# Two tiles of a shared expert moved from a context stage into the following sums stage

## The chip, the cores and the metric

The kernel runs on one core of a Trainium2 chip. The metric is the device time of one execution in microseconds (us). The kernel before took 1562.98 us, the median of three runs that lie between 1562.39 and 1564.65.

## The reference, cut to what matters

The input is 4 sequences of 512 tokens with 512 channels. A half-weighted mixture-of-experts layer, attention, and the same mixture layer again are each added to the running sum:

```python
x = x + 0.5 * ffn(layernorm(x), ...)
x = x + attn(layernorm(x), ...)          # attn adds its own input once more
x = x + 0.5 * ffn(layernorm(x), ...)

# ffn, for the rows x of all 2048 tokens
router_logits = x @ gate_w                       # 64 experts
topk_w, topk_ids = grouped_topk(router_logits, bias)   # 6 experts of 4 of 8 groups
y = routed_moe(x, topk_w, topk_ids, w_gate, w_up, w_down)   # at most 96 tokens per expert
shared = silu(x @ ws_gate) * (x @ ws_up) @ ws_down          # 192 hidden channels, all tokens
return y + shared

# attn: 16 heads of 32 channels, rotary embedding on half of them
scores = einsum('bhqd,bhkd->bhqk', Q, K) / sqrt(32)
ctx = einsum('bhqk,bhkd->bhqd', softmax(scores), V)
return ctx @ W_out + X
```

The change concerns the line `shared`, in the second mixture layer, for one of the four sequences.

## The kernel before, in words

Everything is float32 in tiles of 128 rows; a sequence is four such tiles (TPB = 4). The kernel has three parts: the first mixture layer, the attention of the four sequences, and the second mixture layer with its 64 experts. Sequences are numbered from 0 in the code, so "the second sequence" is `b = 1`.

The attention part (the loop at L1066) has two stages for each sequence, a sums stage and a context stage, of 16 steps each.

- A step of `sums(b)` (L953 on) has four score matmuls `sc` (L962), two maxima on VectorE (L965), four exponentials with row sums on ScalarE (L970). From these the logarithm of each row's sum is formed (`logs`, L935), and transposed in `rows_of_sums` (`ps_m`, L980) at step 16.
- A step of `context(b)` (L1021 on) has four transposed score matmuls `sct` (L992) and four that subtract the logarithms (L996), two exponentials on ScalarE (`pT`, L1003), and the product with the values of the step before (`cx`, L1015).

Between these instructions the other work is threaded in. It stands in a list `work` of pairs, a number and a function (class `Pieces`, L44). Each step takes pieces off its head: `short()` takes a piece whose number is under 1.0, and it stands ahead of the step's exponentials; `long()` takes one short piece if one is at the head, and then one more of any size, behind the exponentials. In a sums stage `long` takes nothing once only two long pieces are left (`keep`), and `work.all()` puts out the rest between the stages, with no score matmuls beside it. `rest` is a long piece that does nothing. A second list, `work.later`, has small VectorE jobs; a sums step does one of them, a context step two.

What is threaded in: in the sums stage of `b`, the output projection of sequence `b-1` (`project`, `po`, L860) and the queries, keys and values of `b+1` (`qkv`, `pq`, L811); the fourth sums stage (`b = 3`) has no next sequence and takes routing work instead. The routing of a finished sequence consists of

- `early_rows` and `scored`: normalised rows `xn` (`route.row`, L295, stored to DRAM on the SP queue), their transposes (`route.turn`), and router scores `lg` (`route.score`, L308); after the last tile's score, the seven parts of `choices` (L319, VectorE, picks the experts) go to `work.later`;
- `gated`: for each of the four tiles, `route.gate` (four `gu` matmuls with the shared expert's weights, L208; a tanh on ScalarE, L211; two VectorE products, L214 and L215), `route.turn_h` (transposes of the hidden tile `sg`, L201, and a ScalarE copy `hT`, L202) and `route.down` (two `so` matmuls, L508, and a VectorE sum into `x`, L509). Tile i is turned and put down in the piece after the one that gates it, and `route.store` hands finished tiles to the SP queue (L516);
- `queued`: turns and puts down the fourth tile, does what is left of `choices`, then `count` (two `pp` matmuls, L405 and L406, that need the chosen masks `M` and `Ms` from VectorE), `digits` (VectorE), `tokens` (ScalarE, L436) and `spread` (`o` matmuls, L447), which build the experts' lists of tokens.

The order on PE, ScalarE and VectorE in this part is the order in which the code issues the work; each engine runs its own stream in order and waits by semaphores. Two pools of PSUM matter: `psS` with three buffers for `sc` and `sct` (a step uses two; in the second and third context stages `cx` takes one of the three), and `psT` with two buffers for all the other matmul results.

In the kernel before, all of sequence 1's routing (`scored(1)`, `gated(1)`, `queued(1)`) is threaded into the third context stage (`b = 2`); the fourth sums stage threads in the projection of sequence 2, two rests, and sequence 2's rows, scores and shared expert; the fourth context stage has two rests and `queued(2)`.

Of the kernel before, what the change touches and what calls it, by code (L numbers as in the profile page):

```python
# [21 lines left out]
TPB = S // P  # L22
# [61 lines left out]
def macaron_kernel(ctx: ExitStack, tc: tile.TileContext, X, ln_w, ln_b, W_in, W_out, gate_w, bias,  # L84
# [156 lines left out]
    def load_pair(layer, n, extra):  # L241


        slot = (extra if (n + (0 if layer else WS)) % (WS + WX) >= WS else wp).tile([P, 4608], F32, tag="w", name="w")
        wg = slot[:, 0:2 * DC * F].rearrange("p (t c f) -> p t c f", t=2, c=DC)
        wu = slot[:, 2 * DC * F:4 * DC * F].rearrange("p (t c f) -> p t c f", t=2, c=DC)
        wd = slot[:, 4 * DC * F:].rearrange("p (k d) -> p k d", k=3)
        two = slice(2 * n, 2 * n + 2)
        loaded[layer, n] = (wg, wu, wd)
        return [lambda: nc.sync.dma_start(wg, w_gate[two].rearrange("t (p c) f -> p t c f", c=DC)),  # L250
                lambda: nc.sync.dma_start(wu, w_up[two].rearrange("t (p c) f -> p t c f", c=DC)),
                lambda: nc.sync.dma_start(wd, w_down[two].rearrange("t f d -> (t f) d").rearrange("(k p) d -> p k d", p=P))]

    def load_now(*args):
        for go in load_pair(*args):
            go()
# [371 lines left out]
    with ExitStack() as s:  # L628
# [4 lines left out]
        with ExitStack() as f:  # L633
            rp = f.enter_context(tc.tile_pool(name="rp0", bufs=2))
            f.enter_context(tc.manual_schedule(engines={mybir.EngineType.SP}))
            xs = []
            for t in range(NT):
                g, i = divmod(t, TPB)
# [14 lines left out]
            for t in range(2 * TPB + 1):  # L653
                g, i = divmod(t, TPB)
# [14 lines left out]
            rest = [go for n in range(WS + WX) for go in load_pair(0, n, extra)]  # L669
# [58 lines left out]
    with ExitStack() as s:  # L728
# [8 lines left out]
        route = Route(1)  # L737
# [11 lines left out]
        xs, stats, qT, kT, v, nmT, keyed = xas, {}, {}, {}, {}, {}, {}  # L749
        work = Pieces()  # L750

        def places(b):
            qT[b] = qp.tile([P, DC, S], F32, tag="qT", name="qT")
            kT[b] = qp.tile([P, DC, S], F32, tag="kT", name="kT")
            v[b] = vp.tile([P, TPB, D], F32, tag="v", name="v")
# [17 lines left out]
        def summed(b):  # L773

            mv = small.tile([P, TPB, 2], F32, tag="mv4", name="mv")
            for i in range(TPB):
                stat_later(b, mv, i)
            steps_later(first(b, mv))
# [75 lines left out]
        def project(b):  # L854
            mv = small.tile([P, TPB, 2], F32, tag="mv4", name="mv")

            def part(q):
                po = psT.tile([P, 512], F32, tag="ps", name="po")
                for c in range(NC):
                    nc.tensor.matmul(po, lhsT=qT[b][:, c, q * P:(q + 1) * P], rhs=win[3][:, c, :],  # L860
                                     start=c == 0, stop=c == NC - 1)
                nc.vector.tensor_add(xs[b][q], xs[b][q], po)
                if b < B - 1:
                    stat_later(b, mv, q)
                    if q == TPB - 1:
                        steps_later(route.ready(b, mv))
            return [(3.4, lambda q=q: part(q)) for q in range(TPB)]

        def early_rows(b):
            def part(i):  # L870
                while (b, i) not in route.stats:
                    work.flush(1)
                route.row(b, xs[b], i)
            return [(0.1, lambda i=i: part(i)) for i in range(2)]

        rest = (1.0, lambda: None)

        def scored(b, chosen):

            def part(i):  # L880
                route.score(b, i)
                if i + 2 < TPB:
                    route.row(b, xs[b], i + 2)
                if i == TPB - 1:
                    steps = route.choices(b)
                    chosen.append(lambda: next(steps, None))
                    work.later[:0] = chosen * 7

            pieces = [(0.5, lambda: route.turn(b, 0)), rest]
            for i in range(TPB):  # L890
                if i + 1 < TPB:
                    pieces.append((0.5, lambda i=i: route.turn(b, i + 1)))
                pieces.append((1.4, lambda i=i: part(i)))
            return pieces

        def gated(b):
            def part(i):
                route.store()
                if i > 0:
                    route.down(b, xs[b], i - 1)  # L900
                route.gate(b, i)

            pieces = []
            for i in range(TPB):
                if i > 0:
                    pieces.append((0.3, lambda i=i: route.turn_h(b, i - 1)))
                pieces.append((4.3, lambda i=i: part(i)))
            return pieces

        def queued(b, chosen):  # L910

            def last():
                route.down(b, xs[b], TPB - 1)
                while work.later and work.later[0] in chosen:
                    work.flush(1)
                route.store()
                route.count(b)

            def digits(i):
                if i > 0:  # L920
                    route.spread(b, i - 2)
                route.digits(b, i)

            pieces = [(0.3, lambda: route.turn_h(b, TPB - 1)), (1.7, last)]
            for i in (0, 2):
                pieces += [(0.6, lambda i=i: digits(i)), (1.0, lambda i=i: route.tokens(b, i)), rest]
            pieces.append((0.6, lambda: route.spread(b, 2)))
            return pieces
# [109 lines left out]
        pieces, following = qkv(0), qkv(1)  # L1038
# [26 lines left out]
        chosen = []  # L1065
        for b in range(B):  # L1066
            if b > 0:
                pieces = project(b - 1)
                if b + 1 < B:
                    places(b + 1)  # L1070
                    following = qkv(b + 1)
                    pieces.insert(3, following.pop(0))
                    work.add(pieces + following[:-5] + early_rows(b - 1) + following[-5:])
                else:
                    work.add(pieces + [rest, rest] + early_rows(b - 1) + scored(b - 1, chosen) + gated(b - 1))
            logs = sums(b, work, 2)
            work.all()
            if b + 2 == B:
                load_now(1, 0, None)
            if b == 0:  # L1080
                summed(2)
                summed(3)
            elif b < B - 1:
                chosen = []
                work.add(scored(b - 1, chosen) + gated(b - 1) + queued(b - 1, chosen))
            else:
                work.add([rest, rest] + queued(b - 1, chosen))
            context(b, work, b in (0, B - 1), logs)
            work.all()
            chosen = []  # L1090
# [90 lines left out]
```

## Time and profile before

The profile is of one execution that took 1569.51 us; the span from its first to its last instruction is 1567.8 us. Busy time of the engines in the stages around the change, and the clock that TensorE was granted, as a share of full speed:

| stretch (us from the start) | stage | length | PE busy | DVE busy | ACT busy | PE clock |
|---|---|---|---|---|---|---|
| 766 to 847 | second context (`b = 1`) | 81 | 80.47 | 26.24 | 38.90 | 0.96 |
| 847 to 941 | third sums | 94 | 90.20 | 62.34 | 70.38 | 0.99 |
| 941 to 1020 | third context (`b = 2`) | 79 | 78.45 | 25.71 | 37.40 | 0.94 |
| 1020 to 1113 | fourth sums (`b = 3`) | 93 | 77.03 | 56.10 | 58.24 | 0.78 |
| 1113 to 1176 | fourth context | 63 | 60.62 | 16.45 | 34.59 | 0.92 |

PE is TensorE's matmuls, DVE is VectorE, ACT is ScalarE, SP is the queue that issues most transfers. A matmul's record is longer when the granted clock is lower, so "busy" grows without more work being done. In a timeline, a row merges neighbouring instructions of one line; a time in square brackets is how long the engine stood idle before the row, with the engine and line that ended the wait.

### The profile page before, as it was taken

To read this page: it belongs to the slowest core of one execution; us is meant where nothing else is said; L and a number is where in the kernel's file an instruction comes from. 1 tells how busy PE (TensorE), PEld (TensorE's weight loads), DVE (VectorE), ACT (ScalarE), POOL (GpSimd) and SP (SyncE) were. 2 spreads that over 40 slices of the span, in tenths; PEclk is the share of its full clock that TensorE was granted. 3 is DMA by queue.
4 is the path that set the end of the run, shared out by engine and by line. 5 is a ranking of instruction groups with operands and counts; after the bars stand their busy time and mean duration, and the time that the engine had idled before them with its cause. 6 is when DMAs were issued, how large, how long until landed. Compare 5 with 4: busy or idle time off the path is not lost.

```text
span 1567.8 us, 23011 instructions
## 1 busy us (share of the span) xinstructions
PE 1407.9 (90%) x9024; PEld 803.2 (51%) x9024; DVE 625.0 (40%) x1572; ACT 594.5 (38%) x1161; POOL 350.7 (22%) x321
## 2 busy tenths in 40 slices
PE   4785999999998998999999999978998899999990
PEld 4553777776753443334443434324334477777760
DVE  7575222211217566177144843375316422122110
ACT  4431121211112487668635774467362112121120
POOL 2001355545434000000000000000000245555535
PEclk9998899999999997999999998986798799999995
DMA  5477699999999300000000020000006389999989
GB/s 195 142 227 256 188 330 330 328 334 337 337 274 176 122 1 1 1 1 1 27 31 1 1 74 21 24 14 20 25 1 240 122 266 333 336 337 328 338 253 122
DMA packets 127036, 254.57 MB, mean 162 GB/s; under 512 B 15801, under 2 KB 32313, under 8 KB 126929
## 3 DMA queue, kind: packets, MB, share of 16 engines
q1 hardware_dynamic: 87216, 192.96, 35.1%
q0 software_dynamic: 39424, 59.97, 17.9%
q8 instruction: 72, 1.18, 0.3%
q14 instruction: 36, 0.29, 0.1%
q10 hardware_dynamic: 288, 0.16, 0.0%
HBM read 202.21 MB, written 56.95 MB: 165 GB/s over the span
## 4 chain that ended last, share of the span: by engine, by line
PE 56%; ACT 5%; DVE 4%; DMA 2%; issue 2%; POOL 1%; SPq 0%; POOLq 0%; ACTq 0%; DVEq 0%
PE pq L811 10%; PE gu L549 6%; PE sct L992 5%; PE sc L962 4%; PE cx L1015 4%; PE sct L996 4%; PE ps_t L201 4%; PE po L860 3%; PE eo L568 3%; PE gu L208 3%; PE so L508 3%; PE gu L553 3%; ACT sc L970 2%; PE eo L571 2%; DMA w<-in_L_ffn_w_up_dram 1%
## 5 line engine op out<-in xcount | busy, mean ns | idle before, releaser
L526 POOL DMA_INDIRECT xr<-xn_d,en x128 | 119.5, 934 | 893.7 <-DVE sg L215 721.2
L549 PE MATMUL gu<-bT,w 128*128 128x96 f32 x2048 | 245.1, 278 | 7.5 <-DMA w<-in_L_ffn_w_up_dram 7.3
L549 PEld LDWEIGHTS gu<-bT,w 128*128 128x128 f32 x2048 | 238.3, 194 | 10.3 <-issue 10.2
L970 ACT ACTIVATE sc<-sc,nmq 128x512 f32<-128x512 f32 x256 | 168.9, 660 | 58.2 <-DVE nmq L965 52.5
L811 PE MATMUL pq<-w,lT 128*128 128x512 f32 x384 | 177.1, 608 | 6.6 <-ACT lT L202 2.7
L965 DVE TENSOR_REDUCE nmq<-sc 128x2 f32<-128x1024 f32 x128 | 151.4, 1220 | 78.3 <-PE sc L962 78.2
L576 POOL DMA_INDIRECT total<-ob,en x96 | 138.6, 1443 | 159.3 <-ACT ob L575 120.4
L575 ACT ACTIVATE ob<-eo,xr 96x512 f32<-96x512 f32 x128 | 80.5, 678 | 185.9 <-PE eo L571 182.6
L560 DVE SCALAR_TENSOR_TENSOR sg<-sg,gu 128x288 f32<-128x288 f32 x64 | 29.0, 454 | 298.6 <-ACT sg L559 204.5
L1003 ACT ACTIVATE pT<-sct 128x1024 f32<-128x1024 f32 x128 | 124.1, 1023 | 58.1 <-PE sct L996 57.9
L559 ACT ACTIVATE sg<-gu 128x288 f32<-128x288 f32 x64 | 26.2, 410 | 314.4 <-PE gu L555 310.5
L568 PE MATMUL eo<-w,hT 128*96 128x512 f32 x256 | 125.3, 612 | 0.0
L202 DVE COPY bT<-ps_t 128x384 f32<-128x384 f32 x128 | 65.5, 552 | 147.4 <-PE ps_t L201 127.3
L811 PEld LDWEIGHTS pq<-w,lT 128*128 128x128 f32 x384 | 70.8, 193 | 95.9 <-issue 79.5
L962 PE MATMUL sc<-kT,qT 32*128 32x512 f32 x512 | 98.1, 719 | 10.4 <-ACT sc L970 9.8
L553 PE MATMUL gu<-bT,w 128*64 128x96 f32 x1024 | 99.9, 252 | 0.0
L555 PE MATMUL gu<-bT,w 128*64 128x96 f32 x1024 | 99.9, 252 | 0.0
L208 PE MATMUL gu<-wsgu,xT 128*128 128x384 f32 x256 | 94.8, 518 | 1.4 <-ACT ob L575 1.4
L992 PE MATMUL sct<-qT,kT 32*128 32x512 f32 x512 | 91.3, 659 | 2.1 <-ACT pT L1003 2.1
L553 PEld LDWEIGHTS gu<-bT,w 128*64 128x64 f32 x1024 | 87.7, 139 | 6.2 <-issue 0.3
L555 PEld LDWEIGHTS gu<-bT,w 128*64 128x64 f32 x1024 | 87.7, 139 | 0.0
L996 PE MATMUL sct<-nmT,pick 4*128 4x512 f32 x512 | 85.4, 614 | 0.0
(162 smaller groups left out, 1649.5 us busy)
## 6 DMA issues: line engine op xcount, KB each, us to landing
w<-in_L_ffn_w_gate_dram SPq DMA_DIRECT2D x64, 768.0 KB
w<-in_L_ffn_w_up_dram SPq DMA_DIRECT2D x64, 768.0 KB
w<-in_L_ffn_w_down_dram SPq DMA_DIRECT2D x64, 768.0 KB
total<-zero SPq DMA_DIRECT2D x39, 256.0 KB
xn_d<-xn SPq DMA_DIRECT2D x32, 256.0 KB
x<-in_L_attn_X_dram SPq DMA_DIRECT2D x16, 256.0 KB
x<-total POOLq DMA_DIRECT2D x16, 256.0 KB
out_dram<-x SPq DMA_DIRECT2D x16, 256.0 KB
```

Of the source, the lines that this page charges most:

```text
L208: nc.tensor.matmul(gu[:rows, :2 * F].rearrange("p (w f) -> p w f", w=2), lhsT=bT[:, c, :], rhs=weights[:, :, c, :], start=c == 0, stop=c = ...
L549: nc.tensor.matmul(g[:, k, :], lhsT=w[:, k, c, f:f + P], rhs=x[:, c, :], start=c == 0, stop=c == DC - 1)
L553: nc.tensor.matmul(g[:FC, 2, :], lhsT=w[:, 0, c, P:F], rhs=xa[:, c, :], start=c == 0, stop=c == DC - 1)
L555: nc.tensor.matmul(g[FC:, 2, :], lhsT=w[:, 1, c, 0:FC], rhs=xb[:, c, :], start=c == 0, stop=c == DC - 1)
L568: nc.tensor.matmul(eos[k][:CAP], lhsT=hT[:, k, :], rhs=wd[:, 2 * k, :], start=True, stop=False)
L576: nc.gpsimd.indirect_dma_start(out=total[layer][k], in_=ob, in_offset=None, out_offset=bass.IndirectOffsetOnAxis(ap=en[:, e:e + 1], axis=0 ...
L811: nc.tensor.matmul(pq, lhsT=lTs[i][:, c, :], rhs=win[n][:, c, :], start=c == 0, stop=c == DC - 1)
L962: nc.tensor.matmul(scs[j // 2][:, j % 2, :], lhsT=qT[b][rows, c, q * P:(q + 1) * P], rhs=kT[b][rows, c, :], start=True, stop=True)
L965: nc.vector.tensor_reduce(nmv[:, q, 2 * pair:2 * pair + 2, c], scs[pair], AX.X, ALU.max, negate=True)
L970: nc.scalar.activation(scs[j // 2][:, j % 2, :], scs[j // 2][:, j % 2, :], AF.Exp, bias=nmq[:, q, j * DH + c:j * DH + c + 1], accum_out=sm ...
L992: nc.tensor.matmul(scs[j // 2][:, j % 2, :], lhsT=kT[b][rows, c, kt * P:(kt + 1) * P], rhs=qT[b][rows, c, :], start=True, stop=False)
L996: nc.tensor.matmul(scs[j // 2][:, j % 2, :], lhsT=pick[rows, c, :], rhs=nmT[b][c // (NC - 1)][rows, :], start=False, stop=True)
```

## The change

The gates of the third and fourth tile of sequence 1, with the turning and putting down of its second, third and fourth tile, leave the third context stage and go into the fourth sums stage, directly behind the projection of sequence 2, in the place of the two rests. For that, `gated` takes a list of tiles, and has the turning and putting down of the fourth tile in itself (it was in `queued`). This last also holds for the other sequences: for sequence 0 in the second context stage, putting down the fourth tile and `count` become two pieces, in two steps; for sequence 2 the fourth tile is turned and put down in the fourth sums stage's list and no longer in the fourth context stage.

```diff
-        def gated(b):
+        def gated(b, tiles=range(TPB)):
             def part(i):
                 route.store()
                 if i > 0:
                     route.down(b, xs[b], i - 1)
                 route.gate(b, i)
 
+            def last():
+                route.down(b, xs[b], TPB - 1)
+                route.store()
+
             pieces = []
-            for i in range(TPB):
+            for i in tiles:
                 if i > 0:
                     pieces.append((0.3, lambda i=i: route.turn_h(b, i - 1)))
                 pieces.append((4.3, lambda i=i: part(i)))
-            return pieces
+            return pieces + ([(0.3, lambda: route.turn_h(b, TPB - 1)), (1.7, last)] if TPB - 1 in tiles else [])
 
         def queued(b, chosen):
 
             def last():
-                route.down(b, xs[b], TPB - 1)
                 while work.later and work.later[0] in chosen:
                     work.flush(1)
                 route.store()
...
-            pieces = [(0.3, lambda: route.turn_h(b, TPB - 1)), (1.7, last)]
+            pieces = [(1.0, last)]
...
-                    work.add(pieces + [rest, rest] + early_rows(b - 1) + scored(b - 1, chosen) + gated(b - 1))
+                    work.add(pieces + gated(b - 2, (2, 3)) + early_rows(b - 1) + scored(b - 1, chosen) + gated(b - 1))
...
-                work.add(scored(b - 1, chosen) + gated(b - 1) + queued(b - 1, chosen))
+                work.add(scored(b - 1, chosen) + gated(b - 1, range(TPB if b == 1 else 2)) + queued(b - 1, chosen))
```

No instruction of the kernel is added or taken away on TensorE, ScalarE, VectorE or the transfer queues; their order changes, and the queue of GpSimd keeps its order.

## The prediction

> **What bounds the kernel now.** First the page's busy shares and its row of slices, then the windows of the stages around the change:
>
> ```profile
> PE 1407.9 (90%) x9024; PEld 803.2 (51%) x9024; DVE 625.0 (40%) x1572; ACT 594.5 (38%) x1161; POOL 350.7 (22%) x321
> ...
> PEclk9998899999999997999999998986798799999995
> ```
>
> ```profile
> 941.00:1020.00 79.00, 78.45 (x486) 32.99 (x486) 25.71 (x81) 37.40 (x51) 0.00 (x0) 0.94 0.06 23
> 1020.00:1113.00 93.00, 77.03 (x266) 36.03 (x262) 56.10 (x95) 58.24 (x150) 0.00 (x0) 0.78 0.05 20
> 1113.00:1176.00 63.00, 60.62 (x428) 22.48 (x420) 16.45 (x53) 34.59 (x41) 0.00 (x0) 0.92 0.02 7
> ```
>
> PE sets the end everywhere but in the fourth sums stage (1020 to 1113): there it is idle for 16 of 93 us, and its clock is down to 0.78, while the third context stage (941 to 1020) keeps it busy for 78.45 of 79. So the change takes PE work out of a stage where PE is the bound and puts it where PE waits. How much of the idle time can be filled is seen in PE's timeline: first the steps of the third context stage with gated tiles, then the sums stage, then the start of the fourth context stage.
>
> ```profile
> 974.34 1.14 PE L992 MATMUL sct<-qT,kT 32*128 32x512 f32 x8
> 977.62 1.98 PE L508 MATMUL so<-wsd,hT 96*128 96x512 f32 x4
> 979.45 2.75 PE L208 MATMUL gu<-wsgu,xT 128*128 128x384 f32 x8
> 995.31 1.14 PE L992 MATMUL sct<-qT,kT 32*128 32x512 f32 x8
> ...
> 1038.49 1.99 PE L962 MATMUL sc<-kT,qT 32*128 32x512 f32 x12
> 1051.57 1.12 PE L201 MATMUL ps_t<-ident,xn 128*128 128x128 f32 x4 [3.87 <-ACT xn L295]
> 1080.22 4.14 PE L208 MATMUL gu<-wsgu,xT 128*128 128x384 f32 x8
> 1084.28 1.14 PE L962 MATMUL sc<-kT,qT 32*128 32x512 f32 x8
> 1090.93 1.14 PE L962 MATMUL sc<-kT,qT 32*128 32x512 f32 x8
> 1096.61 1.09 PE L980 MATMUL ps_m<-ident,nmq 128*128 128x128 f32 x4 [3.99 <-DVE nmq L950]
> 1105.53 0.43 PE L201 MATMUL ps_t<-ident,sg 128*96 128x128 f32 x2 [1.20 <-DVE sg L215]
> 1106.41 3.49 PE L508 MATMUL so<-wsd,hT 96*128 96x512 f32 x4 [0.46 <-ACT hT L202]
> 1112.60 1.14 PE L992 MATMUL sct<-qT,kT 32*128 32x512 f32 x8
> 1123.81 0.66 PE L201 MATMUL ps_t<-ident,sg 128*96 128x128 f32 x2
> 1126.27 2.44 PE L508 MATMUL so<-wsd,hT 96*128 96x512 f32 x4
> 1129.49 0.27 PE L405 MATMUL pp<-M,before 128*128 128x256 bf16 x1 [0.78 <-DVE x L509]
> ```
>
> Two steps are to be seen. The rests (from 1038.49) end in a wait of 3.87 us for the first normalised row, whose statistics are not ready; and from there on the same work takes longer: `gu` 4.14 us against 2.75, `so` 3.49 against 1.98. Windows cut at those places show why:
>
> ```profile
> 1059.00:1082.85 23.85, 22.53 (x80) 14.38 (x79) 11.08 (x12) 17.98 (x47) 0.00 (x0) 0.50 0.06 22
> 1082.85:1096.50 13.65, 9.06 (x37) 3.74 (x35) 11.53 (x33) 8.58 (x25) 0.00 (x0) 1.00 0.05 19
> 1117.00:1127.20 10.20, 10.20 (x39) 2.37 (x36) 2.02 (x9) 4.38 (x7) 0.00 (x0) 0.50 0.05 13
> ```
>
> The granted clock is 0.50 while rows are turned and scored, 1.00 while tiles are gated, and 0.50 again at the start of the context stage.
>
> **The change part by part** (times of the profiled execution).
>
> *Third context stage.* Before, three steps, from the `sct` at 974.34 to that at 995.31, hold what leaves (two `gu`, three turns, three `so`) and `count`: 20.97 us. After, one of them is left, with `sct` and `cx` (3.0 us, to 977.35) and `count`; `pp` waits for the masks, which VectorE's timeline has ready at 978.58 already now, so 1.1 us of waiting and 0.4 for `pp`: 4.4 us. Two plain steps come back at the end of the stage; such steps last 3.17 (995.31 to 998.48) and 3.83 us (to the `sct` at 1002.31), as PSUM holds only three `sct` buffers and `cx` has one: 7.0. With `choices` ending behind `count`'s wait, `digits` come 1.8 us later against the step, and `tokens` hold ScalarE for about 0.7. Gain: 20.97 - 4.4 - 7.0 - 0.7 = 8.9. Bounds: 8 (plain steps of 3.83 and twice the token wait) to 11 (plain steps of 3.04 as at 1156 to 1168 in the fourth context stage, no token wait).
>
> *Second context stage.* `count` moves to the next step; the last `spread` moves into the last step, where PE waits for the final exponentials anyway (0.18 at 843.50, and a `cx` of 1.97 us instead of 1.07). I take -0.5; bounds -1.2 (one whole `o` group, 1.09, hidden) and +1.5 (a `count` that waits as above).
>
> *Fourth sums stage, front.* Before, from the `sc` at 1038.49 to the first exponential behind the first row (ScalarE, 1051.32): 12.8 us. After, the two steps with a turn, `so` and `gu` last as the like step from 1084.28 to 1090.93, 6.65 each, PE-bound (ScalarE needs 2.95 + 0.37 + 0.33 in it, VectorE 2.4 + 1.4 + 0.9). The third has `sc`, turn, copy and `so` alone: 1.1 + 0.1 + 0.4 + 0.5 + 1.9 = 4.0. Then the eighth `sc` and its first maximum, and the row in front of its exponentials, 2.6 more; the statistics are done a step earlier, so no 3.87 wait. Sum 19.9: cost 7.0. The scoring steps that follow keep their period (6.02 us from the `sc` at 1061.14 to that at 1067.16), at half clock, since transposes and `lg` behind idle steps are what ran at 0.50 before. Bounds: 4.5 (turned rows start at full clock) to 8.5 (a third step of 5.5).
>
> *Its tail.* Before, from the second gate's end (1091.0) to the first `sct`, 1112.60: 21.6 us, with one sums step and a wait of 3.99 for the logarithms. After, one step of the stage fewer is left and one tile more. The logarithms stand behind the second gate's tanh and products: 0.35 + 0.75 + 0.45 = 1.6; `ps_m` 0.65; `sc` 1.1; then turn 0.55, copy 0.46, `so` and `gu` 4.6; twice wait for products 1.2, turn and copy 0.9, and `so` and `gu` 4.6, or `so` alone 2.0: 1.6 + 0.65 + 1.1 + 5.6 + 6.7 + 4.1 = 19.7. Half clock cost this tail 3.0 before (`sc` +0.95, `ps_m` +0.45, `so` +1.5, `gu` +0.2); I put half of it on: 21.2, a gain of 0.4. Bounds: -1.9 to +2.6 (two `so` more at 3.49).
>
> *Fourth context stage.* A turn, an `so` and the 0.78 wait of `pp` for its buffer go: 0.66 + 2.44 + 0.78 = 3.9. Four parts of `choices` instead of three stand behind the last sum `x`; they take 0.9 + 4.8 us (VectorE, 1102.02 to 1102.89 and 1113.73 to 1118.50), the log of the last column waits for them and the second exponentials for that: 0.7 given back. `count`, ten us behind the first `sct`, finds its masks (five us). Gain 3.1; bounds 2 to 6.3 (the third step, 9.7 us from 1120.08 to 1129.80, at 3.4 as with full clock).
>
> *Queues.* Three stores of `x` (256 KB or less each) now stand before sequence 2's row stores on SP, and the masks' weights `wt` before two of them; the transfers run at 20 GB/s in these stages, a row buffer is used again only two steps later, and the readers are the experts after 1243. Nothing, unless a row waited for its buffer: then 1 us at one step. POOL's order stays.
>
> Sum: -8.9 - 0.5 + 7.0 - 0.4 - 3.1 = -5.9. Behind the attention all shifts as it is. 1569.51 - 5.9 = 1563.6; the median of the runs is 0.9958 of the profiled execution: **1557.1**.
>
> The Trainium skill ("TensorE: Matmul & The Clock Gate", "Why this matters for your kernels") says to leave no PE gap over some 3 us, or the clock halves. The 3.87 wait that goes is such a gap, so by that rule the scoring would stay at full clock and the sum would be the second rival's -12. The row from 1059 to 1082.85 speaks against it: 0.50 throughout, with PE waits of at most 1.5 us before it and 0.7 in it.
>
> **The rivals.**
>
> 1. As summed: 1557, within 1551 to 1561 by its own clock windows. Chance 0.50.
> 2. *The clock stays full from the gated steps through scoring and tail.* Two scoring periods lose 0.5 each in the turn (1.12 to 0.65), the turn before them 0.6, the next two steps 1.2 and 1.0, the first `gu` 1.4, the tail 1.5: 6 us or so more, 1551. For it: full clock at 1082.85 to 1096.5. Against it: the row above. Chance 0.22.
> 3. *Nothing is filled.* The third context stage gains its least (8), the sums stage costs its most (8.5 + 2.6) and the last gains 2: -8 + 11.1 - 2 - 0.5, about 0.6 us slower, 1562 to 1564. It decides where the front's steps wait on ScalarE, as the `sc` at 1042.57 did for 2.09 us. Chance 0.17.
> 4. *Slower: the half clock lasts from scoring into the gating and the tail.* The tail is a chain of turn, copy, `so`, `gu`, with waits of 1.2 and 0.46. If these keep the clock at 0.50, four `so` cost 1.5 more, three `gu` 1.4, three `sc` 0.95: 13, less the 1.5 counted, so -5.9 + 11.5 = +5.6, 1568.6. It decides from 9.0 us of such loss on (to outdo 5.9 + 3.1). For it: the row at 1105.53 and the 3.49 behind it. Against it: 1.00 from 1082.85 over the same steps, waits included. Chance 0.11. The Trainium skill (same page, "A second HAM failure mode: psum-queue depth-cycling") tells of such small idles between groups that make the clock swing; no run here shows it at full load.
>
> **How the numbers follow.** 0.2% is 3.1 us, about what a measurement tells from no change. Case 1 is faster but for the upper tenth of its range (0.46 of 0.50); case 2 is faster (0.22); case 3 is no change but for a little (0.15); case 4 slower. Faster 0.68, same 0.19, slower 0.13. The range leaves out the far end of case 2 and case 4: the bounds sum to -15.9 and +3.1, and I take 1548.5 to 1564.
>
> **What would show it.** Third context stage some 9 us shorter, `pp` with a wait of about 1 us; three gated steps behind `po` in the fourth sums stage, no wait before the first turned row; a clock of 0.5 during scoring; `ps_m` waiting some 1.6 instead of 3.99; from the last `po` to the first `sct` about 6.6 us more; no turn or `so` in the fourth context stage. It is wrong if the sums stage grows by more than 9 us, or if `pp` waits several us, or if the clock takes another course.

## The result and the profile after

The changed kernel took 1559.36 us, the median of 22 executions (1554.45 to 1572.91). In the same comparison the kernel before took 1566.9 us (22 executions, 1557.19 to 1584.88). The ratio is 0.9962, with a 95% interval of 0.9946 to 0.9979: about 6 us faster. It leaves out executions that lie over 1.5% above the fastest of their kernel, so it is nearer to 1 than the ratio of the two medians. The profiled execution of the changed kernel took 1554.45 us.

First the page of the changed kernel: busy shares and the row of granted clocks.

```profile
PE 1397.2 (90%) x9024; PEld 797.1 (51%) x9024; DVE 625.6 (40%) x1572; ACT 594.5 (38%) x1161; POOL 351.3 (23%) x321
...
PEclk9897899999999997999999999996898899999995
```

PE is busy for 10.7 us less with the same 9024 matmuls. So some of the difference between the two profiles is clock, and one profile against one profile mixes it with what the change does. The windows of the three stages, this time cut at their own first score matmuls, and of the scoring steps (us, then busy time of PE, PEld, DVE, ACT, POOL, the granted clock, the transfers' share and GB/s):

```profile
926.90:1003.60 76.70, 74.79 (x498) 29.90 (x496) 22.60 (x76) 41.15 (x54) 0.00 (x0) 0.96 0.08 28
1003.60:1103.70 100.10, 88.67 (x305) 41.19 (x304) 59.63 (x101) 60.23 (x156) 0.00 (x0) 0.83 0.07 27
1103.70:1164.50 60.80, 59.20 (x424) 22.76 (x424) 16.61 (x54) 34.30 (x39) 0.00 (x0) 0.92 0.02 7
1043.70:1074.40 30.70, 28.38 (x94) 16.34 (x93) 14.89 (x15) 23.74 (x61) 0.00 (x0) 0.50 0.07 26
```

The third context stage is shorter, the fourth sums stage longer, the fourth context stage shorter. The last row is the scoring: 0.50 throughout, as before. Cut the same way in both kernels, from the first score matmul of a stage to that of the next (the fourth context stage to its last `cx`), and with the changed kernel profiled a second time in another execution:

| profile | second context | third context | fourth sums | fourth context |
|---|---|---|---|---|
| before | 87.62 | 87.07 | 92.91 | 63.52 |
| after | 86.96 | 76.61 | 100.14 | 60.76 |
| after, second profile | 87.96 | 73.71 | 100.09 | 57.28 |

The two profiles of the changed kernel differ by 2.9 and 3.5 us in the two context stages, with the same code: in the first one TensorE ran at half clock for 6.8 and 10.2 us of them, in the second for none. Before had 10.2 and 10.2 us. The spans of the two first profiles differ by 15.0 us, and only 6.6 of them lie between the start of the second context stage and the last `cx`; 5.0 lie ahead and 3.4 behind, where nothing was moved. The second profile of the changed kernel has these two stretches 8.5 and 4.0 us longer than the first. So the stages, and not the spans, tell what the change does.

Now the places that were priced, in PE's timeline of the changed kernel (start, duration, line, and in brackets the idle time before the row):

```profile
964.97 1.14 PE L995 MATMUL sct<-qT,kT 32*128 32x512 f32 x8
968.26 0.27 PE L405 MATMUL pp<-M,before 128*128 128x256 bf16 x1 [0.29 <-DVE M L380]
969.03 0.27 PE L406 MATMUL pp<-Ms,ones 128*128 128x256 bf16 x1 [0.50 <-DVE Ms L385]
969.23 1.14 PE L995 MATMUL sct<-qT,kT 32*128 32x512 f32 x8
1003.56 1.14 PE L965 MATMUL sc<-kT,qT 32*128 32x512 f32 x8
...
1022.36 1.14 PE L965 MATMUL sc<-kT,qT 32*128 32x512 f32 x8
1028.81 1.14 PE L965 MATMUL sc<-kT,qT 32*128 32x512 f32 x8
1035.46 1.14 PE L965 MATMUL sc<-kT,qT 32*128 32x512 f32 x8
1039.52 1.14 PE L965 MATMUL sc<-kT,qT 32*128 32x512 f32 x8
1042.16 0.66 PE L201 MATMUL ps_t<-ident,xn 128*128 128x128 f32 x4 [1.50 <-ACT xn L295]
...
1071.92 4.07 PE L208 MATMUL gu<-wsgu,xT 128*128 128x384 f32 x8
1075.91 1.14 PE L965 MATMUL sc<-kT,qT 32*128 32x512 f32 x8
1079.89 2.75 PE L208 MATMUL gu<-wsgu,xT 128*128 128x384 f32 x8
1084.20 0.66 PE L983 MATMUL ps_m<-ident,nmq 128*128 128x128 f32 x4 [1.56 <-DVE nmq L953]
1088.56 2.75 PE L208 MATMUL gu<-wsgu,xT 128*128 128x384 f32 x8
1093.39 2.33 PE L508 MATMUL so<-wsd,hT 96*128 96x512 f32 x4 [0.46 <-ACT hT L202]
1095.52 4.13 PE L208 MATMUL gu<-wsgu,xT 128*128 128x384 f32 x8
1100.84 0.42 PE L201 MATMUL ps_t<-ident,sg 128*96 128x128 f32 x2 [1.20 <-DVE sg L215]
```

To be seen: `pp` waits 0.79 us in all for the masks; the gated steps of sequence 1 last 6.45 and 6.65 us, the third, with a turn and a put-down alone, 4.06; the wait ahead of the first turned row is 1.50 us instead of 3.87; `ps_m` waits 1.56 instead of 3.99. The first `gu` at 1071.92 still starts at half clock (4.07 us for 2.75), and one half-clock window falls into the tail (2.33 and 4.13). The list of PE's waits in the fourth sums and context stages (1003.6 to 1164) ends the search for a new one. The four longest of its eight entries:

```profile
PE so L508 <- ACT hT L202: 3.3, 7, 0.5
PE ps_t L201 <- ACT xn L295: 2.8, 3, 1.5
PE ps_t L201 <- DVE sg L215: 2.4, 2, 1.2
PE ps_m L983 <- DVE nmq L953: 1.6, 1, 1.6
```

(total us, times, longest.) No transfer is among the eight causes, so the stores that stand earlier on SP cost PE nothing.

### The profile page after: what moved, and what is told of

Same layout as the page of the kernel before. It is cut to its first block, busy times and chain, and to the rows that moved or that the text cites. A ratio compares the mean times of both kernels' runs of the same rounds, so it can differ in the third digit from the quotient of the medians.

```text
span 1552.7 us, 23015 instructions
## 1 busy us (share of the span) xinstructions
PE 1397.2 (90%) x9024; PEld 797.1 (51%) x9024; DVE 625.6 (40%) x1572; ACT 594.5 (38%) x1161; POOL 351.3 (23%) x321
## 4 chain that ended last, share of the span: by engine, by line
PE 55%; ACT 5%; DVE 4%; DMA 3%; issue 2%; POOL 1%; POOLq 0%; SPq 0%; ACTq 0%; DVEq 0%
PE pq L811 10%; PE gu L549 6%; PE sct L995 5%; PE sc L965 4%; PE cx L1018 4%; PE sct L999 4%; PE ps_t L201 4%; PE po L860 3%; PE eo L568 3%; PE gu L208 3%; PE so L508 3%; PE gu L553 2%; PE eo L571 2%; ACT sc L973 2%; DMA w<-in_L_ffn_w_up_dram 1%
## 5 line engine op out<-in xcount | busy, mean ns | idle before, releaser
L995 PE MATMUL sct<-qT,kT 32*128 32x512 f32 x512 | 95.7, 669 | 2.2 <-ACT pT L1006 2.1
```

The source lines that it names most:

```text
L995: nc.tensor.matmul(scs[j // 2][:, j % 2, :], lhsT=kT[b][rows, c, kt * P:(kt + 1) * P], rhs=qT[b][rows, c, :], start=True, stop=False)
```

## The experiments

The theory was the prediction's own: a tile costs less in the sums stage's gaps than in a context stage where PE is the bound, and the wait for the first row, the wait of `ps_m` and the tail say how much less. The rivals were that splitting the fourth tile off `count`, not the move, carries the gain; that the two dropped rests carry it; and that the scoring's half clock decides. Diffs are against the changed kernel unless said otherwise; line numbers of `sums` and `context` move by a few lines with the edits.

**The move alone.** The fourth tile of sequences 0 and 2 stays in `queued`, ahead of `count`.

```diff
-        def gated(b, tiles=range(TPB)):
+        def gated(b, tiles=range(TPB), down=False):
...
-            return pieces + ([(0.3, lambda: route.turn_h(b, TPB - 1)), (1.7, last)] if TPB - 1 in tiles else [])
+            return pieces + ([(0.3, lambda: route.turn_h(b, TPB - 1)), (1.7, last)] if down else [])
...
             def last():
+                if b != 1:
+                    route.down(b, xs[b], TPB - 1)
...
-            pieces = [(1.0, last)]
+            pieces = [(1.0, last)] if b == 1 else [(0.3, lambda: route.turn_h(b, TPB - 1)), (1.7, last)]
...
-                    work.add(pieces + gated(b - 2, (2, 3)) + early_rows(b - 1) + scored(b - 1, chosen) + gated(b - 1))
+                    work.add(pieces + gated(b - 2, (2, 3), True) + early_rows(b - 1) + scored(b - 1, chosen) + gated(b - 1))
```

> Only the move of sequence 1's tiles; sequences 0 and 2 keep the turn and down of their fourth tile in one piece with count. If the move makes the gain: third context stage 77 to 78 us instead of 87, fourth sums stage 96 (3 more than before: 7 in front, 4 less in the tail, which ends one turn and one so earlier), fourth context stage as before with 0.7 more, together about -5 us. If the split makes it (rival), about 0.

Measured: 1560.85 us (median of 12), ratio 1.0007 [0.9973, 1.0042]. The times lie in two groups, seven from 1554.5 to 1561.1 and five from 1571.2 to 1575.9; the profiled execution (1561.06) is of the lower one. The granted clock of the whole execution is 0.936 to 0.947 in the lower group and 0.926 to 0.932 in the upper one; the kernel before, in the same job, had 0.933 to 0.943 in 34 of its 35 executions, and a median of 1564.62. The lower group's median, 1557.18, is 7.4 us under that, but this group was picked out after the fact. In the profile the third context stage lasts 77.42 us, with the same 10.2 us of half clock as before: 9.65 less. The fourth sums stage lasts 95.08 (+2.2), the fourth context stage 64.21 (+0.7). That is -6.8 in these stages. An execution of the upper group was not profiled, so for the whole kernel this run says nothing firm, while for the third context stage it gives the price at an equal clock.

**The split alone**, the two tiles staying in the third context stage; run in two jobs, on two chips.

```diff
-                    work.add(pieces + gated(b - 2, (2, 3)) + early_rows(b - 1) + scored(b - 1, chosen) + gated(b - 1))
+                    work.add(pieces + [rest, rest] + early_rows(b - 1) + scored(b - 1, chosen) + gated(b - 1))
...
-                work.add(scored(b - 1, chosen) + gated(b - 1, range(TPB if b == 1 else 2)) + queued(b - 1, chosen))
+                work.add(scored(b - 1, chosen) + gated(b - 1) + queued(b - 1, chosen))
```

> Only the split: gated has the fourth tile's turn and down in itself, for all sequences, but sequence 1 stays whole in the third context stage and the two rests stay. If the gain comes from moving sequence 1's tiles into PE's idle time, little of it is seen here: second context stage -0.7 us (as measured in the changed kernel), fourth context stage -2.8, and in the fourth sums stage one more gated piece is drawn into the steps, so that its tail costs 1 to 2 more; about -2 us against the kernel before, third context stage unchanged at 87 us. If the split makes the gain (rival), the whole -6 us is seen here.

> The kernel with only the split, once more, for a second profile: its times lay in two groups, 1547 to 1556 and 1560 to 1568 us, and the profile was of the upper one (1562.84). If the groups come from the granted clock, an execution of the lower group shows fewer us at 0.50 in the fourth sums stage, the context stages or behind them, and the rest of the stages alike to 0.2 us; if they come from something else, the stages differ at equal clock.

Measured: 0.995 [0.9922, 0.9977] and 0.9956 [0.992, 0.9992], medians 1554.33 and 1561.45: by itself as much as the whole change, so that by the time of the whole kernel this rival stands. The stages of the first profile explain a part, 3.8 us: second context -0.65, third context -0.1, fourth sums -0.65 although a turn and two `so` were added there, fourth context -2.4 in spite of 2.5 us more of half clock. Two things stand behind the sums stage's figure. Its list has one long piece more, so that its fifteenth step, which before had nothing to take (two pieces are kept back), gates the third tile beside the exponentials; and `ps_m` then waits 1.56 us instead of 3.99. And half clock lengthened the rows of the tail, from `ps_m` to the first `sct`, by 3.2 us before (`sc` 2.09 for 1.14, `so` 3.49 for 1.98 and three smaller ones) and by 0.4 here (`so` 2.42); with that taken off, the stage is 2.2 us longer than before, not 0.65 shorter. Again the times lie in two groups (1547 to 1556 and 1560 to 1569), both profiles are of the upper one, and the clocks of the two groups overlap (0.934 to 0.947 and 0.926 to 0.941). The lower group stays unexplained, and with it most of what the split gains.

**Is it the kept pieces?** The kernel before, with nothing kept back in the fourth sums stage:

```diff
-            logs = sums(b, work, 2)
+            logs = sums(b, work, 2 if b < B - 1 else 0)
```

> The kernel before, where the fourth sums stage alone keeps no long piece back (keep 0 instead of 2): two gated pieces of the last sequence but one come into steps 15 and 16 that stood behind them. If the split gained because its extra piece drew a gated piece out of the tail into the steps, the same is seen here without the split: no wait of 3.99 us ahead of ps_m but 1.6, fourth sums stage 87 to 89 us instead of 93, third and fourth context stages as before, -4 to -6 us. If the split gained by what it moves (the turn and so out of the fourth context stage), nothing is gained here.

Measured: the fourth sums stage lasts 86.57 us, 6.3 less than before (expected 87 to 89). Its tail in PE's timeline:

```profile
1088.70 2.75 PE L208 MATMUL gu<-wsgu,xT 128*128 128x384 f32 x8
...
1095.36 2.75 PE L208 MATMUL gu<-wsgu,xT 128*128 128x384 f32 x8
1099.66 0.65 PE L980 MATMUL ps_m<-ident,nmq 128*128 128x128 f32 x4 [1.56 <-DVE nmq L950]
...
1104.02 2.75 PE L208 MATMUL gu<-wsgu,xT 128*128 128x384 f32 x8
1106.69 1.14 PE L992 MATMUL sct<-qT,kT 32*128 32x512 f32 x8
```

Three gates stand ahead of `ps_m` (the first began ahead of these rows) and one behind it, where before two and two did. That is the same wait and the same order of gates as in the split, which has one turn and one put-down more behind them, and it is reached without any move. Of the 6.3 us, 3.2 are the half clock that fell into the tail before and not into this one; the other 3.1 go with the list, whose length, against the kept pieces and the sixteen steps, decides what falls into the tail. The whole kernel's ratio, 0.9972 [0.9938, 1.0006], is less sure, as its times scatter from 1547 to 1599 us.

**The two rests.** First the changed kernel with the rests kept behind the two tiles:

```diff
-                    work.add(pieces + gated(b - 2, (2, 3)) + early_rows(b - 1) + scored(b - 1, chosen) + gated(b - 1))
+                    work.add(pieces + gated(b - 2, (2, 3)) + [rest, rest] + early_rows(b - 1) + scored(b - 1, chosen) + gated(b - 1))
```

> The changed kernel with the two rests put back, behind the moved tiles. If the gain is that the moved work takes the place of two idle steps, it is gone: two steps of 3.2 us come back, and two gated pieces are pushed behind the last step, where they cost 6.7 us instead of 6.65 with their step: fourth sums stage 106 to 109 us instead of 100, 0 to +3 us against the kernel before. If it is enough to relieve the third context stage, wherever the work goes in the sums stage (rival), -6 us stays.

Measured: 1568.03 us, 1.0023 [1.0005, 1.0042]; the fourth sums stage 105.11 us, 5.0 more than in the changed kernel. The whole gain is gone: two steps that take nothing push two pieces into the tail, so that all four gates stand behind `ps_m`, where no exponentials run beside them.

Then the kernel before without its rests:

```diff
-                    work.add(pieces + [rest, rest] + early_rows(b - 1) + scored(b - 1, chosen) + gated(b - 1))
+                    work.add(pieces + early_rows(b - 1) + scored(b - 1, chosen) + gated(b - 1))
```

> The kernel before with the two rests simply left out, nothing moved. If idle steps must be filled with PE work to gain, this brings little: the first row waits for its statistics, the stage has its 16 steps all the same, and two steps without a piece come at its end: fourth sums stage 90 to 95 us against 93, -1 us in all. If the rests were the loss by themselves (rival), fourth sums stage 87 us and -6 us.

Measured: 1571.63 us, 1.0036 [0.9999, 1.0074]. Dropping the rests does not bring what the change brings. PE's timeline shows both reasons:

```profile
1060.71 1.12 PE L201 MATMUL ps_t<-ident,xn 128*128 128x128 f32 x4 [7.13 <-ACT xn L295]
...
1101.46 0.42 PE L201 MATMUL ps_t<-ident,sg 128*96 128x128 f32 x2
...
1113.12 1.09 PE L980 MATMUL ps_m<-ident,nmq 128*128 128x128 f32 x4 [3.34 <-DVE nmq L950]
```

The first row is waited for 7.13 us instead of 3.87, so that the front gets 4.8 us shorter and not the 8.1 that the two steps took. And the stage has its sixteen steps all the same, so that two without a piece come at its end: from the last turn ahead of `ps_m` to `ps_m` itself it is 11.66 us against 4.41. The fourth sums stage lasts 96.74 (+3.8, expected -3 to +2), some of it clock, as 47.8 us of it are at half clock and 41.0 were before. The profiled execution (1579.28) is one of six of this kernel at a clock of 0.913 to 0.929; the other six, at 0.935 to 0.941, have a median of 1561.8, 2.8 us under before. So a small gain is not excluded. In the profile the third context stage, whose code is that of before, took 98.80 us; the section on the hardware comes back to it.

**The scoring's clock.** Filler matmuls (128 rows by 512 columns, their result unread) are put behind the turn and the score of each row, so that the clock stays up; they add PE work. There are 16 of them (the expectation counts twelve), and they take 15.2 us of PE in the profile.

```diff
+        def fill(n):
+            ps = psT.tile([P, 512], F32, tag="ps", name="fill")
+            for c in range(n):
+                nc.tensor.matmul(ps, lhsT=wsgu[:, 0, c, 0:P], rhs=win[3][:, c, :], start=c == 0, stop=c == n - 1)
+
-        def scored(b, chosen):
+        def scored(b, chosen, filled=False):
...
                 route.score(b, i)
+                if filled:
+                    fill(2)
...
-            pieces = [(0.5, lambda: route.turn(b, 0)), rest]
+            def turn0():
+                route.turn(b, 0)
+                if filled:
+                    fill(4)
+
+            pieces = [(0.5, turn0), (1.0, lambda: fill(4)) if filled else rest]
...
-                    work.add(pieces + gated(b - 2, (2, 3)) + early_rows(b - 1) + scored(b - 1, chosen) + gated(b - 1))
+                    work.add(pieces + gated(b - 2, (2, 3)) + early_rows(b - 1) + scored(b - 1, chosen, True) + gated(b - 1))
```

> The changed kernel with twelve extra matmuls of 128x128 by 128x512 (two groups of four beside the first turned row and in the rest, two behind each score of the last sequence but one) whose result nobody reads, in the fourth sums stage. If half clock there comes from PE having too little to do (second rival of the prediction), the clock stays at 1.00, the scoring steps last 5.5 us instead of 6.02, and the stage takes 95 to 97 us instead of 100. If the clock stays at 0.50 all the same, each scoring step, where PE has 5.6 of 6.02 us, gets 1.1 to 1.5 us longer and the stage takes 104 to 107.

Measured: 1561.57 us, 0.9984 [0.9952, 1.0016]. The window of the scoring steps:

```profile
1053.20:1081.50 28.30, 25.77 (x127) 12.55 (x126) 14.71 (x15) 21.58 (x57) 0.00 (x0) 1.00 0.07 28
```

The clock is 1.00 now, and yet a step takes 5.6 to 5.7 us instead of 6.02. What closes the loop of a scoring step is seen on PE and ScalarE, first in the changed kernel:

```profile
1056.22 1.11 PE L201 MATMUL ps_t<-ident,xn 128*128 128x128 f32 x4 [0.66 <-ACT xn L295]
1057.37 0.59 ACT L202 COPY xT<-ps_t 128x512 f32<-128x512 f32 x1 [1.20 <-PE ps_t L201]
```

then with the fillers:

```profile
1070.33 0.66 PE L201 MATMUL ps_t<-ident,xn 128*128 128x128 f32 x4 [1.18 <-ACT xn L295]
1071.02 0.59 ACT L202 COPY xT<-ps_t 128x512 f32<-128x512 f32 x1 [0.75 <-PE ps_t L201]
```

PE waits for the next row from ScalarE even with the fillers in, and ScalarE's one wait in the step is the one for the turn. So of PE's work the turn alone is in the loop: it gets 0.45 us shorter, and so does ScalarE's wait. From the `sc` of the third moved step to that behind the first gate it is 38.96 us against 40.45 (1042.53 to 1081.49, and 1035.46 to 1075.91). These 1.5 us are a net figure and no price of the clock: the three steps from the first turned row on, with ten of the fillers, are 2.4 us longer, the two scoring steps 0.7 shorter, and the stretch from there to behind the first gate 3.1 shorter. The tail gives it back (half clock falls there, with `gu` of 3.91 and 3.97 us, and the first gated tile is waited for 1.55 us): the stage lasts 101.78 us, which neither side had expected.

**How many tiles.** Three tiles moved, and one:

```diff
-                    work.add(pieces + gated(b - 2, (2, 3)) + early_rows(b - 1) + scored(b - 1, chosen) + gated(b - 1))
+                    work.add(pieces + gated(b - 2, (1, 2, 3)) + early_rows(b - 1) + scored(b - 1, chosen) + gated(b - 1))
...
-                work.add(scored(b - 1, chosen) + gated(b - 1, range(TPB if b == 1 else 2)) + queued(b - 1, chosen))
+                work.add(scored(b - 1, chosen) + gated(b - 1, range(TPB if b == 1 else 1)) + queued(b - 1, chosen))
```

> The changed kernel with the second tile moved too, so three gated pieces behind the projection. If the move pays only as far as it takes the place of idle steps, the third tile loses: third context stage 74 to 76 us instead of 76.6 (7.8 leave, a plain step of 3.5 comes back, and count waits about 3 us for its masks), fourth sums stage 106 to 107 instead of 100 (6.65 more, at full price); 4 to 5 us more than the changed kernel, about -2 us against the kernel before. If every tile moved gains alike (rival), -8 to -9 us against before.

Measured: 1568.39 us, 1.0041 [1.0005, 1.0078], slower than before by some 6 us, where about 2 us less was expected. The third context stage lasts 78.67 us, 20.5 of them at half clock. The fourth sums stage lasts 106.25 us, 6.1 more than with two tiles, and `pp` waits longer in the third context stage:

```profile
968.22 0.33 PE L405 MATMUL pp<-M,before 128*128 128x256 bf16 x1 [2.34 <-DVE M L380]
```

```diff
-                    work.add(pieces + gated(b - 2, (2, 3)) + early_rows(b - 1) + scored(b - 1, chosen) + gated(b - 1))
+                    work.add(pieces + gated(b - 2, (3,)) + early_rows(b - 1) + scored(b - 1, chosen) + gated(b - 1))
...
-                work.add(scored(b - 1, chosen) + gated(b - 1, range(TPB if b == 1 else 2)) + queued(b - 1, chosen))
+                work.add(scored(b - 1, chosen) + gated(b - 1, range(TPB if b == 1 else 3)) + queued(b - 1, chosen))
```

> The changed kernel with the fourth tile alone moved. Third context stage 80 to 81 us (4.3 more than the changed kernel's 76.6, a gated step for a plain one), no wait of count; fourth sums stage 96 to 98, as one step less stands in front of the first row, which waits about 2 us for its statistics; fourth context stage as in the changed kernel: -3 to -5 us against the kernel before. If the wait for the statistics is what the move fills (rival), 2 us more are lost and it gains nothing.

> One tile moved, once more, beside the changed kernel on the same chip: third context stage 80, fourth sums stage 95, fourth context stage 56 to 61 as its start falls into half clock or not; 1551 to 1557 us.

Measured: 0.9912 [0.9882, 0.9942] and 0.9942 [0.992, 0.9964], medians 1553.38 and 1554.2. One tile is at least as good as two. In PE's timeline of the first of these runs:

```profile
1045.63 1.12 PE L201 MATMUL ps_t<-ident,xn 128*128 128x128 f32 x4 [4.98 <-ACT xn L295]
...
1090.03 2.75 PE L208 MATMUL gu<-wsgu,xT 128*128 128x384 f32 x8
1094.34 0.66 PE L983 MATMUL ps_m<-ident,nmq 128*128 128x128 f32 x4 [1.56 <-DVE nmq L953]
...
1103.52 1.98 PE L508 MATMUL so<-wsd,hT 96*128 96x512 f32 x4 [0.46 <-ACT hT L202]
1105.44 1.14 PE L995 MATMUL sct<-qT,kT 32*128 32x512 f32 x8
```

The row is waited for longer (4.98 us) than with two tiles (1.50), and still the stage is 4.9 us shorter (95.25): its list is one piece shorter, so the third gate (1090.03) stands ahead of `ps_m` and not behind it. Of the 4.9 us, 1.7 are clock: in the changed kernel half clock lengthened two rows of the tail (`so` 2.33 and `gu` 4.13), here none.

**One piece less.** If that is so, the changed kernel should gain the same by losing the rest that `scored` puts behind its first turn, for sequence 2 alone:

```diff
-            pieces = [(0.5, lambda: route.turn(b, 0)), rest]
+            pieces = [(0.5, lambda: route.turn(b, 0))] + ([rest] if b < B - 2 else [])
```

> The changed kernel without the rest inside scored for the last sequence but one, so that its long pieces in the fourth sums stage are 16 for 16 steps, as with one tile moved, not 17. If the second moved tile pays less because the list no longer fits the steps and a gated piece falls behind the last one, the stage is 95 to 96 us instead of 100, third context stage 77, together -11 to -15 us against the kernel before. If the moved tile costs its PE time in any place (rival), 100 us stay.

Measured: 1552.38 us, 0.9934 [0.9907, 0.9961] (one of its twelve executions took 2001.52 us, at a mean clock of 0.657 instead of 0.937 to 0.948; why, nothing shows); the fourth sums stage 95.13 us (expected 95 to 96), 5.0 less than in the changed kernel, about 1 of it clock in the tail, with the third gate ahead of `ps_m` again. The whole is about 10 us under before, just short of the 11 to 15 expected. In the same job, on the same chip, the changed kernel was run once more:

> The changed kernel once more, for a second profile. By the sum of the prediction the third context stage is 77 to 78 us and the fourth sums stage 99 to 100; the first profile's 76.6 had full clock at the start of the third context stage, where the kernel before had 10.2 us of half clock (3.7 us). If that is chance, the third context stage is up to 4 us longer here; if the change makes it, it is 76.6 again.

Measured: 1557.66 us, 0.9965 [0.9937, 0.9992]. One tile (1554.2) and one rest less (1552.38) are ahead of it by 3.5 and 5.3 us in the medians. The intervals overlap; what is sure is the 5 us in the stage.

**The account at an equal clock.** What half clock costs in a context stage can be read from the two profiles of the changed kernel: 60.76 - 57.28 = 3.5 us for 10.2 us of it, 0.34 us per us. In the third context stage the same two profiles give 2.9 us for 6.8, 0.43 per us. With 0.34 taken off the third and fourth context stages (before 10.2 and 10.2 us at half clock, split alone 10.2 and 12.7, one tile 6.8 and 0, two tiles 6.8 and 10.2, three tiles 20.5 and 10.2), an estimate of the difference to before, in us; the fourth sums stage stands as measured:

| tiles moved | second context | third context | fourth sums | fourth context | sum | measured ratio |
|---|---|---|---|---|---|---|
| none (split alone) | -0.7 | -0.1 | -0.7 | -3.3 | -4.7 | 0.995, 0.9956 |
| one | -0.7 | -6.1 | +2.3 | -3.7 | -8.0 | 0.9912, 0.9942 |
| two (the change) | -0.7 | -9.3 | +7.2 | -2.8 | -5.5 | 0.9962, 0.9965 |
| three | -0.6 | -11.9 | +13.3 | -0.5 | +0.2 | 1.0041 |

The first tile takes 6 us out of the third context stage and puts 3 into the sums stage; the second 3.2 against 4.9; the third 2.6 against 6.1 (3.8 with 0.43 per us). With the lengthened rows of the sums stage's tail taken off as well (3.2 us before, 0.4 with the split alone, none with one tile, 1.7 with two and with three), the stage is 2.2, 5.6, 8.7 and 14.8 us longer than before, and the second tile costs 3.2 there, no more than it takes out. The sums then are -1.9, -4.8, -4.0 and +1.7. The ratios stand for about -7 us for the split, -9 to -14 for one tile, -6 for two and +6 for three: the last three come in the same order, but the amounts are not reached, and the split's least of all.

## Why the prediction was right, by its steps

The sum of -5.9 us of 1569.5, a ratio of 0.9962, is what was measured, and the steps hold one by one to 1.6 us or better, so it is not a sum of large errors that cancel. That it agrees to the last digit is luck: the interval is 2.6 us wide to either side, and the stages of the profile sum to -6.6. 1557.1 was worked out for a kernel before of 1562.98; that one took 1566.9 over all 22 executions, and the changed one 1559.36. The upper end of the bounds, +3.1, does not come out of the parts, which sum to +2.6; nothing hangs on it.

- *Third context stage, 8.9.* The profile has 10.5, the move alone at an equal clock 9.65. The step with `count` took 4.26 us (964.97 to 969.23; priced 4.4), with 0.79 of waiting (1.1). The plain steps that come back were priced at 7.0, and 0.7 for `tokens`: in the second profile of the changed kernel, at full clock, the stretch behind `count` grew from 24.38 to 31.42 us, 7.0 in all, so the 0.7 was too much. In the first profile it took 34.33, as two half-clock windows fell on it.
- *Second context stage, 0.5.* Measured 0.66.
- *Front of the fourth sums stage, +7.0.* From the `sc` behind the last `po` to the exponentials behind the first row 19.65 us (1022.36 to 1042.01) against 12.83: +6.8. The first turned row is still waited for 1.50 us, where none was forecast, but that lies within the 2.6 us priced from the eighth `sc` on. The scoring kept its half clock and its period of 6.02 us; scoring to second gate took 0.9 more, which was not priced.
- *Tail, -0.4.* From the second gate's end to the first `sct` 21.05 us against 21.6: -0.55. Half of the half clock's cost was put on it, and one window fell there.
- *Fourth context stage, -3.1.* Measured -2.8 in the profiles, both with 10.2 us of half clock at the stage's start. ScalarE waits 2.55 us for the logarithm's argument instead of 2.05: 0.5 given back, for 0.7 priced.
- *Queues, nothing.* No wait of PE on a transfer.

The second rival's mechanism did not come (0.50 during scoring). Its price is not refuted: it put 1.0 us on two scoring periods and 3.6 on the two steps and the `gu` behind them, and the filled kernel shows 0.7 and 3.1, fillers included. For the rest of its 6 us that run has no clean figure. The Trainium skill ("TensorE: Matmul & The Clock Gate", "Why this matters for your kernels") advises to leave no PE gap over about 3 us. In the changed kernel the longest wait of PE in these two stages is 1.6 us, and the clock is 0.50 from 1043.7 to 1074.4 all the same, so the rule's condition was met here without its effect, as the prediction took it. In the kernel before, too, the clock had fallen at 1045.30, ahead of the 3.87 us wait, which began at 1047.70. The third and fourth rivals are out with their conditions: the steps did fill the gap, and the gates and the tail ran mostly at full clock.

What the prediction did not see, though its sum did not need it: the parts are not additive. It took the split as a small side effect. In time the split alone is worth as much as the whole, and its stages show only a part of that, so how much of the change's gain is the move's stays open; what is shown is what each does in the stages. The split lengthens the list by the one piece that fills the empty fifteenth step; the two tiles in place of two rests add one more, and push a gate into the tail again. "One step of the stage fewer is left and one tile more" is that effect, priced rightly but not recognised as avoidable.

## What to carry to other kernels

Moving work from a stage where an engine is the bound to one where it waits pays only up to the wait: price each piece apart. In the two stages the first tile here took out 6 us for 3, the third 2.6 for 6.1. Where work is threaded by a list into a fixed number of steps, count the pieces against the steps before and after, and see which piece falls behind the last step; that was worth 3 to 4 us here with the clock taken off, 5 to 6 as measured. And before a slow clock is given a price, see which work of the slowed engine is in the loop: in a scoring step it was the turn alone, 0.45 of 6.02 us.

## What the runs showed of the hardware

*A fully busy PE does not lift the half clock by itself.* In the profile of the kernel before without its rests, in the third context stage, a window in a long half-clock stretch (which reaches from 941.4 to 979.0):

```profile
945.00:982.00 37.00, 37.00 (x158) 16.18 (x157) 5.88 (x21) 12.79 (x19) 0.00 (x0) 0.54 0.04 15
```

and its end in PE's timeline:

```profile
974.64 1.94 PE L1015 MATMUL cx<-pT,v 128*32 128x512 f32 x8
976.50 4.08 PE L208 MATMUL gu<-wsgu,xT 128*128 128x384 f32 x8
980.51 1.14 PE L992 MATMUL sct<-qT,kT 32*128 32x512 f32 x8
```

PE is busy for 37.00 of 37 us at a mean clock of 0.54, and the clock comes back within the first `gu`. The scoring's half clock, too, ends within the first `gu` in before (1080.22) and after (1071.92), and it did not set in where 128x128x512 fillers stand between (1.00). But the clock also comes back without a wide matmul. In the changed kernel's first profile one half-clock window lies in the third context stage among `sct` and `cx` alone, and the next 17 us, which hold these and two groups of `o`, run at full clock:

```profile
975.40:978.85 3.45, 3.45 (x19) 0.88 (x14) 0.00 (x0) 1.17 (x2) 0.00 (x0) 0.51 0.00 0
978.85:995.80 16.95, 16.73 (x140) 6.54 (x132) 4.99 (x11) 9.67 (x11) 0.00 (x0) 1.00 0.00 1
```

So neither PE's busy share nor the width of the matmuls decides alone in these rows, and what does is open. The Trainium skill (same page, Part 1) says that one busy window of some 3.4 us brings full speed; the short window agrees with it, the long stretch, with some ten such windows, does not. The same part's free-running window of 3413 ns agrees: within each of the profiles all changes of the clock lie on one grid of 3.41 us.

*The half clock comes by execution.* The same code at the start of a context stage runs at half clock for 10.2 us in one execution and for none in another (the changed kernel's fourth context stage), for 3.5 us; in the stage of the long stretch it took 37.5 us where before had 10.2, and the stage 98.80 us against 87.07: 11.7 more for 27.3. The kernel before, too, spread from 1557 to 1585 us; in its three later sets of 35 executions, those of 1575 us and more had a mean clock of 0.922 to 0.932, the others 0.933 to 0.943. Why an execution falls into it is open. With 12 executions of a kernel the intervals here are 0.4 to 0.8% wide, and stages of two profiles can be compared only with their clock windows beside them.
